# A planner's prices for the attention heads, and the place of the second image's attention and projections, in a two-layer vision kernel

## The chip, the cores and the metric

The kernel runs on one core of a Trainium2 chip. The metric is the device time of one execution in microseconds, as a median of several runs. Engines are named as the profile names them: PE (matrix products), DVE (vector), ACT (scalar, activations), POOL (GpSimd), SP (the queue that issues the DMAs).

## The reference

Two images of 48 x 48 positions with 768 channels, all in fp32, pass through two layers with a residual each:

```
x = x + attention(gn(x))       # 12 heads of 64; each position sees a 7 x 7 neighbourhood
x = x + mamba(gn(x))           # a selective scan over the 2304 positions, forwards and backwards
```

`gn` normalizes over 32 groups of channels and needs the sums over a whole image before the first position can be normalized. The attention computes q, k and v with a 768 x 2304 weight, masked softmax scores, the weighted sum, and an output product. The second layer projects each position to 1536 channels (u) and 1536 gates (z), convolves u with four taps in either direction, projects u to 48 + 16 + 16 values (a step size, B and C), and runs for each of the 1536 channels and 16 states the recurrence `h = exp(d*A)*h + d*u*B`, `y = sum(h*C)`, once over the positions in order and once in reverse. The sum of both, gated by `silu(z)`, goes through an output product of 1536 x 768.

## The kernel before

**The main work.** The scan is cut into 24 passes (2 images x 2 directions x 6 chunks of 384 positions), and each pass into 12 tiles of 128 channels: 288 *channel tiles*, numbered 0 to 287, image 1 from 144. One tile (`scan`, lines 1209 to 1389) has four groups of four states. For each group, `first` (L1254) fills a buffer with d*u*B, on DVE or POOL, whichever the planner finds sooner free; ACT computes exp(d*A) (L1276); DVE runs two scans over two states each (L1287); POOL multiplies by C (L1302); PE adds the states up by transposing into a PSUM bank (L1319); ACT takes the result out (L1345). `deltas_of` prepares three tiles at a time, with a POOL product at L1204.

**The jobs beside it.** Image 0's attention and the projections of its first chunk come ahead of tile 0. All else is laid beside the scans: image 0's other projections, image 1's attention, image 1's projections (`in_proj`: PE products, three DVE taps per tile and direction at L964, ACT silu at L990), the products for B and C (`x_proj`, which stores them to DRAM as `xdf` and `xdb`), and the output products (`out_proj`).

**The planner.** No instruction is issued when its Python line runs. `add(engine, ns, fn, key, r, w, job=...)` records a step with an engine, a planned duration in ns, what it reads and writes, and a *key*: the number of the channel tile beside which it belongs. `Order.run` then plays the steps through: each engine takes the step that can start first by the planned durations, ties going to the lower key, and a step whose key is more than 2.5 above the oldest unfinished main step is not yet open. The order that comes out is the program order of each engine, and SP's order of DMAs with it. On the chip the engines are in order and synchronized by semaphores. So a planned duration changes no instruction; it changes where instructions stand. If PE is planned to be idle for more than 800 ns in a scan, the planner fills the gap with idle transposes (L1520, `idle`), which keep PE running and compute nothing that is used.

**The prices.** `act(n, p) = 60 + 90p + 0.833n` and `dve(n) = 55 + 1.042n` ns, plus an amount by hand; a PE step's price is multiplied by 1.04 ahead of tile 0 and by 1.05 from there.

**The heads.** `heads` (L769 to L900) does one pair of heads for two blocks of 64 queries: scores on PE (L784), per block masked scores on DVE (L794) and exponentials on ACT (L800), reciprocals on DVE (L815), the scaling of the probabilities (L843 on ACT in image 1, L849 on DVE in image 0), their transposes on PE (L825), the copy out of PSUM (L831), the product with v (L879) and the copy of the result (L893). There are 108 such calls per image. `job` is true for image 1, whose attention lies beside the scans. The output product of the attention is `mm_ao`, followed on DVE by the residual sum (L712) and the statistics for the second group norm (L717).

**The places.** `attention(b, start, end, ...)` spreads its six blocks of rows evenly between two keys, and the second group norm has the key `end`. The chunks of `in_proj` of image 1 have their keys from `P1` in fixed steps; chunk i spans 10 tiles, its `x_proj` stands behind it, and the forward scan of chunk i starts at tile 144 + 12 i. A chunk's scan loads its `dt` and its B and C from `xdf`; these DMAs stand on SP's queue.

Of the kernel before, what the change touches and what calls it, by code (L numbers as in the profile page):

```python
# [16 lines left out]
P = 128  # L17
# [13 lines left out]
NKEY = WR * WC  # L31
KR = 7
KCH = tuple((r * WC, KR * WC) for r in range(0, WR, KR))
NK = len(KCH)
UU = 2
# [215 lines left out]
def tile_kernel(  # L251
# [3 lines left out]
    nc = tc.nc  # L255
# [99 lines left out]
    def dve(n):  # L355
        return 55 + n * 1.042
# [177 lines left out]
    def attention(b, start, end, job, T):  # L534
# [234 lines left out]
        def heads(n, p, i, u, kcs, ks, qs, vs, vat, mask, to, key):  # L769


            sc, pt = one("s", n), one("pt", n)
            pr = sb("pr", [P, UU, NKEY], n, parts=UU)
            pT = sb("pT", [P, UU, NK, P], n, parts=UU)
            sm = sb("sm", [P, 2 * UU], n, parts=2 * UU)
            grid = lambda h, kc: ks[h, i * WR * HW : (i + 1) * WR * HW].rearrange("p (r w) -> p r w", w=HW)[:, :, kc : kc + WC]
            scv = lambda v: bank(sc, UU * NKEY)[:, v * NKEY : (v + 1) * NKEY]

            def scores():
                for v in range(UU):  # L780
                    for j in range(2):
                        h = slice(j * E, (j + 1) * E)
                        at = (u * UU + v) * NQ
                        nc.tensor.matmul(  # L784
                            scv(v)[j * NQ : (j + 1) * NQ], qs[h, i, at : at + NQ], grid(h, kcs[v]),
                            start=True, stop=True,
                        )

            add("PE", mm(UU, NKEY) * 1.15, scores, key, r=[(ks, 0), qs], w=[sc, pr], **S)
            for v in range(UU):  # L790

                def masked(v=v):

                    nc.vector.tensor_tensor_reduce(  # L794
                        pr[:, v, :], scv(v), mask[:, v * NKEY : (v + 1) * NKEY], -1.0, 3.0e38,
                        ALU.add, ALU.min, sm[:, v : v + 1],
                    )

                def exponentials(v=v):
                    nc.scalar.activation(  # L800
                        pr[:, v, :], pr[:, v, :], AF.Exp, bias=sm[:, v : v + 1], scale=-1.0,
                        accum_out=sm[:, UU + v : UU + v + 1],
                    )

                add("DVE", dve(NKEY) + 160, masked, key, r=[sc, mask], w=[(pr, v), (sm, v)], **S)
                add(
                    "ACT", act(NKEY, 1) + 230, exponentials, key, r=[(pr, v), (sm, v)],
                    w=[(pr, v), (sm, UU + v)], **S,
                )

                if v == UU - 1 or not job:
                    of = range(UU if job else UU + v, UU + v + 1)
                    add(
                        "DVE", 198,
                        lambda of=of: nc.vector.reciprocal(  # L815
                            sm[:, of.start : of.stop], sm[:, of.start : of.stop]
                        ),
                        key, r=[(sm, of)], w=[(sm, of)], **S,
                    )

            def turned(vs):
                for v in vs:
                    for k, (c0, nk) in enumerate(KCH):
                        x = (v * NK + k) * P
                        nc.tensor.transpose(  # L825
                            bank(pt, UU * NK * P)[:nk, x : x + P], pr[:, v, c0 : c0 + nk], ident
                        )

            def taken(vs, copy):
                nk = KCH[0][1]  # L830
                copy(  # L831
                    pT[:nk, vs.start : vs.stop],
                    bank(pt, UU * NK * P)[:nk, vs.start * NK * P : vs.stop * NK * P].rearrange(
                        "p (v k q) -> p v k q", k=NK, q=P
                    ),
                )

            for v in range(UU):
                if job:

                    add(
                        "ACT", act(NKEY, 1) + 40,
                        lambda v=v: nc.scalar.mul(pr[:, v, :], pr[:, v, :], sm[:, UU + v : UU + v + 1]),  # L843
                        key, r=[(pr, v), (sm, UU + v)], w=[(pr, v)], **S,
                    )
                else:
                    add(
                        "DVE", 300,
                        lambda v=v: nc.vector.tensor_scalar_mul(  # L849
                            pr[:, v, :], pr[:, v, :], sm[:, UU + v : UU + v + 1]  # L850
                        ),
                        key, r=[(pr, v), (sm, UU + v)], w=[(pr, v)], **S,
                    )
            if job:
                add("PE", UU * NK * 110 + 60, lambda: turned(range(UU)), key, r=[pr], w=[pt, pT], **S)
                add(
                    "ACT", act(UU * NK * P) + 30, lambda: taken(range(UU), nc.scalar.copy), key, r=[pt],
                    w=[pT], **S,
                )
            else:  # L860
                for v in range(UU):
                    add(
                        "PE", NK * 120 + 60, lambda v=v: turned([v]), key,
                        r=[(pr, v), *([pt] if v else [])], w=[pt, (pT, v)], **S,
                    )
                for v, (eng, copy) in enumerate((("ACT", nc.scalar.copy), ("DVE", nc.vector.tensor_copy))):
                    add(
                        eng, act(NK * P) + 60, lambda v=v, copy=copy: taken(range(v, v + 1), copy), key,
                        r=[pt], w=[(pT, v)], **S,
                    )  # L870
            po = ps(tag("po", p), f"po{n}")

            def weighted():

                for v in range(UU):
                    for k, (c0, nk) in enumerate(KCH):
                        for j in range(2):
                            e0 = i * P + j * E
                            nc.tensor.matmul(  # L879
                                po[j * E : (j + 1) * E, v * NQ : (v + 1) * NQ],  # L880
                                vat(v, k, nk, e0, e0 + E), pT[:nk, v, k, j * NQ : (j + 1) * NQ],
                                start=k == 0, stop=k == NK - 1,
                            )

            marks["pv"] = add(
                "PE", 900, weighted, key, r=[*((x[0], x[1]) for x in vs), pT], w=[po, to], **S
            )
            o, oi = to

            def kept():  # L890
                copy = nc.scalar.copy if job else nc.vector.tensor_copy
                w0 = u * UU * QC
                copy(  # L893
                    o[:, oi, :]
                    .rearrange("p (r w) -> p r w", w=HW)[:, :, w0 : w0 + UU * QC]
                    .rearrange("p r (v c) -> p v r c", c=QC),
                    po[:, : UU * NQ].rearrange("p (v r c) -> p v r c", v=UU, r=QR),
                )

            add("ACT" if job else "DVE", act(P) + 60, kept, key, r=[po], w=[to], **S)  # L900

        project(0)
        for t in range(NTB):
# [5 lines left out]
    def in_proj(b, i, start, end, conv=True, gate=True, nk=KB, tags=("uz",), banks=("mm",), proj=None):  # L909
# [78 lines left out]
        def finish(k0, nk, uz, dsts, key):  # L988
            def silu():
                nc.scalar.activation(uz[:, :, :, :cl], uz[:, :, :, :cl], AF.Silu)  # L990
                nc.scalar.preload_act_table_set("natural_log_exp_and_others")

            add("ACT", 2600 + act(len(dsts) * nk * cl), silu, key, r=[uz], w=[uz], job=True)
            for s, dst in enumerate(dsts):
                add(
                    "SP", 400,
                    lambda s=s, dst=dst: nc.sync.dma_start(
                        rows_of(dst, k0, nk, l0, cl), uz[:, s, :, :cl]
                    ),
                    key + 0.1, r=[(uz, range(s * nk, (s + 1) * nk))],  # L1000
                    w=[(dst, cols(l0, cl, k0, nk))], job=True, size=nk * P * cl * 4,
                )
# [154 lines left out]
    def deltas_of(ch, k0, x):  # L1157
# [38 lines left out]
        for j in range(KB):  # L1196
# [3 lines left out]
                at + 0.03 + 0.25 * j, [(u, j)], [vts[j]], early=EARLY,  # L1200
            )
            add(
                "POOL", 960,
                lambda j=j: nc.gpsimd.tensor_mul(u[:, j, h], dl[:, j, c], u[:, j, h]), at + 0.06 + 0.25 * j,  # L1204
                [(dl, j), (u, j)], [(u, j)], early=EARLY,
            )
# [239 lines left out]
    LATE = 4  # L1446
    FIRM = 4.0
    HEAD = ("bc4", "bc5", "bc6", "bc7", "bc0", "bc1")
    A0, A1, P1 = (-56, -16), (50, 118), 118
    norms, norms0, stats = [], [], []  # L1450
    for b in range(nb):
        s0 = stats_of(b, A0[0] - 2 + 20 * b, b > 0, ("stage",) if b else ("xc", "uz"))
# [4 lines left out]
    for b in range(nb):  # L1457
# [1 line left out]
        if b:  # L1459
            attention(b, *A1, True, BESIDE)  # L1460
        for i in range(NCH):
            start = P1 + 12 * i if b else 9 * (i - 1) - 4
            end = start + (ND - 2 if b else 8)


# [105 lines left out]
```

## Time and profile before

| | |
|---|---|
| median of three runs | 7049.78 us (7040.85 to 7054.37) |
| the profiled execution | 7040.0 us, of which the span of the core is 7038.2 us |
| first scan tile's start | about 1020 us |
| tiles 0 to 287 | about 1020 to 7007 us |
| what follows (last output product) | 31 us |
| busy over the span | PE 89%, DVE 85%, POOL 78%, ACT 69% |
| granted PE clock, mean | 0.976 |
| idle transposes L1520 | 5124 |

In the profile a view of stretches gives each engine's busy time between two points of the execution. The points used here are the moments at which ACT takes out every twelfth tile's result (L1345), so a stretch is one pass of twelve tiles: 1301.4 us is the end of tile 11, 2841.6 that of tile 83, 3700.1 that of tile 119. A view of waits tells for each instruction that came after idle time which other instruction released it. PE's busy time counts pipelined matmuls by modelled ends, so it is close to full in many places where PE could still take work. An fp32 matmul of the program shows as two instructions in the trace, except for transposes.

### The profile page before, as it was taken

Reading aid. Unit: us, or ns where it says so; the run is one execution under the profiler, and the core shown is the slowest. Engines: PE = TensorE matmul, PEld = TensorE weight load, DVE = VectorE, ACT = ScalarE, POOL = GpSimd, SP = SyncE. Lnnn points to the kernel's source line nnn. Section 1 sums busy time; section 2 is a strip of 40 time slices with the busy share of each in tenths; the row PEclk is TensorE's granted clock in tenths of the full one; section 3 lists DMA queues with packets and bytes.
Section 4 is the critical chain, followed back from the end, with each engine's and each line's share of the span. In section 5 each row is a group of like instructions: output and inputs, shape, how many; then the busy total and the mean of one; then the engine's idle time right before and its main releaser. Section 6 shows DMA issues by size and latency. Waiting matters only on the chain. (4 is left out here: it accounts for less than half of the span.)

```text
span 7038.2 us, 108877 instructions
## 1 busy us (share of the span) xinstructions
PE 6280.1 (89%) x40140; PEld 4878.2 (69%) x40140; DVE 5990.5 (85%) x6102; ACT 4851.3 (69%) x10516; POOL 5468.5 (78%) x1958
## 2 busy tenths in 40 slices
PE   8999899899899989899988888888888898999888
PEld 5666656666667767666766666666678887777777
DVE  1343459999999989878899999999999999999998
ACT  1222248878887777677877777788876667777774
POOL 0000019898889989777889999999999999999997
PEclk9999999999999999999999999999999999999999
DMA  6666454544565455555542443343466676655553
GB/s 194 185 214 190 143 174 131 153 137 133 162 190 162 148 165 166 161 175 155 179 152 87 137 138 89 95 143 114 139 179 191 175 218 198 192 176 160 163 171 104
DMA packets 1348293, 1115.48 MB, mean 158 GB/s; under 512 B 137840, under 2 KB 1338000, under 8 KB 1347728
## 3 DMA queue, kind: packets, MB, share of 16 engines
q1 hardware_dynamic: 1347760, 1108.50, 52.6%
q8 instruction: 318, 5.21, 0.3%
q14 instruction: 215, 1.76, 0.1%
HBM read 895.34 MB, written 213.57 MB: 158 GB/s over the span
## 5 line engine op out<-in xcount | busy, mean ns | idle before, releaser
L1287 DVE TENSOR_TENSOR_SCAN hb<-da,hb 128x772 f32<-128x772 f32 x2304 | 3923.6, 1749 | 200.1 <-ACT da L1276 148.8
L1302 POOL TENSOR_TENSOR hb<-hb,bc 128x1536 f32<-128x1536 f32 x1152 | 3652.7, 3186 | 379.4 <-DVE hb L1287 287.9
L1276 ACT ACTIVATE da<-dlt,A 128x384 f32<-128x384 f32 x4608 | 2677.4, 584 | 962.5 <-DVE hb L1287 884.9
L1319 PE MATMUL py<-ident,hb 128*128 128x128 f32 x13824 | 1750.0, 279 | 313.5 <-POOL hb L1302 306.6
L1319 PEld LDWEIGHTS py<-ident,hb 128*128 128x128 f32 x13824 | 1566.1, 143 | 570.5 <-POOL hb L1302 471.7
L1254 POOL TENSOR_TENSOR hb<-u,bc 128x1544 f32<-128x1544 f32 x502 | 1606.8, 3203 | 48.7 <-PE py L1319 42.6
L1254 DVE TENSOR_TENSOR hb<-du,bc 128x1544 f32<-128x1544 f32 x650 | 1131.3, 1746 | 37.3 <-ACT du L1231 27.5
L1204 POOL TENSOR_TENSOR u<-dlt,u 128x384 f32<-128x384 f32 x288 | 263.6, 917 | 478.0 <-ACT dlt L1191 386.9
L1520 PE MATMUL py<-ident 128*128 128x128 f32 x5124 | 630.8, 277 | 0.0
L387 PE MATMUL mm_xin<-xc,w_x 128*128 128x390 f32 x1656 | 592.6, 501 | 29.8 <-DVE uz_u L964 12.6
L387 PE MATMUL mm_z<-xc,w_z 128*128 128x384 f32 x1728 | 607.6, 492 | 6.3 <-ACT dlt L1186 3.8
L1520 PEld LDWEIGHTS py<-ident 128*128 128x128 f32 x5124 | 586.8, 143 | 17.3 <-issue 13.6
L387 PE MATMUL mm_out<-stage_y,w_o 128*128 128x192 f32 x3168 | 558.0, 330 | 18.9 <-DMA w_o<-in_w_opT 6.5
L387 PEld LDWEIGHTS mm_out<-stage_y,w_o 128*128 128x128 f32 x3168 | 519.0, 193 | 30.5 <-ACT dlt L1186 10.6
L930 POOL MEMSET xc<- 128x18 f32 x4 | 0.5, 118 | 630.0 <-PE mm_v L387 630.0
L964 DVE SCALAR_TENSOR_TENSOR uz_u<-mm_xin,conv_w,uz_u 128x384 f32<-128x384 f32 x792 | 427.9, 610 | 45.6 <-ACT uz_u L957 44.0
L387 PEld LDWEIGHTS mm_xin<-xc,w_x 128*128 128x128 f32 x1656 | 306.3, 193 | 230.2 <-issue 28.8
L387 PE MATMUL mm_qk<-xc_xn,w_qk 128*128 128x384 f32 x1296 | 452.8, 495 | 8.7 <-DVE sm L794 2.6
L387 PEld LDWEIGHTS mm_z<-xc,w_z 128*128 128x128 f32 x1728 | 314.8, 192 | 192.4 <-issue 9.4
L387 PEld LDWEIGHTS mm_qk<-xc_xn,w_qk 128*128 128x128 f32 x1296 | 238.6, 192 | 161.8 <-issue 15.9
L1260 ACT COPY bc<-state 128x8 f32<-128x8 f32 x960 | 183.0, 196 | 143.9 <-DVE hb L1254 68.3
L800 ACT ACTIVATE pr<-pr,sm 128x196 f32<-128x196 f32 x432 | 194.0, 450 | 126.4 <-DVE sm L794 124.8
(163 smaller groups left out, 6454.8 us busy)
## 6 DMA issues: line engine op xcount, KB each, us to landing
w_o<-in_w_opT SPq DMA_DIRECT2D x264, 384.0 KB
bc<-xdf SPq DMA_DIRECT2D x96, 768.0 KB
bc<-xdb SPq DMA_DIRECT2D x96, 768.0 KB
w_qk<-in_w_qkv SPq DMA_DIRECT2D x144, 384.0 KB
w_x<-in_w_inT SPq DMA_DIRECT2D x144, 384.0 KB
w_z<-in_w_inT SPq DMA_DIRECT2D x144, 384.0 KB
w_ao<-in_w_out SPq DMA_DIRECT2D x72, 384.0 KB
u<-uf SPq DMA_DIRECT2D x48, 576.0 KB
```

Of the source, the lines that this page charges most:

```text
L387: nc.tensor.matmul(acc[:m, o0 : o0 + cl], wb[:, wi, wo : wo + m], xb[:, xi, xo : xo + cl], start=c == 0, stop=c == n - 1,)
L800: nc.scalar.activation(pr[:, v, :], pr[:, v, :], AF.Exp, bias=sm[:, v : v + 1], scale=-1.0, accum_out=sm[:, UU + v : UU + v + 1],)
L930: nc.gpsimd.memset(xc[:, :, : a - lo], 0.0)
L964: nc.vector.scalar_tensor_tensor(u, px[:, at[j] : at[j] + cl], q["conv_w"][:, k, j : j + 1], u, ALU.mult, ALU.add,)
L1204: lambda j=j: nc.gpsimd.tensor_mul(u[:, j, h], dl[:, j, c], u[:, j, h]), at + 0.06 + 0.25 * j,
L1254: on.tensor_mul(cells(hb, SG), by.unsqueeze(1).to_broadcast([P, SG, W]), bc[g].ap)
L1260: "ACT", 98, lambda: nc.scalar.copy(bc[g][:, :, ends], was), now - 0.4,
L1276: lambda: nc.scalar.activation(cells(da, 2)[:, j % 2, h], dl[:, jd, c], AF.Exp, scale=q["A"][:, k, i : i + 1]),
L1287: lambda: nc.vector.tensor_tensor_scan(flip(hb[at2]), flip(da[:, : 2 * W]), flip(hb[at2]), 0.0, ALU.mult, ALU.add),
L1302: lambda: nc.gpsimd.tensor_mul(cells(hb, SG)[:, :, h], cells(hb, SG)[:, :, h], bc[NSG + g][:, :, c]),
L1319: nc.tensor.matmul(py[:tp, t * P : (t + 1) * P], cells(hb, SG)[:, j, h][:, tb[t]], ident, start=False, stop=g == NSG - 1 and j == SG - 1 a ...
L1520: nc.tensor.matmul(marks["py"][:, CL : CL + P], ident, ident, start=False, stop=False, is_transpose=True, skip_group_check=True,)
```

## The change

Two kinds of numbers in the planner's input change. First, prices of the attention's steps: masked scores 419 to 281 ns, exponentials 543 to 443, the reciprocals 198 to 70 (image 1) or 150 (image 0), the scaling on ACT 353 to 348, the copy of the transposes in image 1 516 to 486, the product with v 900 to 640 (image 1) or 750 (image 0), the copy of its result 227 to 167 on ACT and 227 to 230 on DVE. Beside them, every silu of the projections is priced 150 ns higher, and the POOL product at L1204 850 instead of 960 ns. Second, places: image 1's attention is keyed from tile 46 to tile 124 instead of 50 to 118, its group norm therefore at 124, and the projections of its six chunks start at keys 124, 135, 146, 157, 168, 179 instead of 118, 130, 142, 154, 166, 178.

```diff
-                add("DVE", dve(NKEY) + 160, masked, key, r=[sc, mask], w=[(pr, v), (sm, v)], **S)
+                add("DVE", dve(NKEY) + 22, masked, key, r=[sc, mask], w=[(pr, v), (sm, v)], **S)
                 add(
-                    "ACT", act(NKEY, 1) + 230, exponentials, key, r=[(pr, v), (sm, v)],
+                    "ACT", act(NKEY, 1) + 130, exponentials, key, r=[(pr, v), (sm, v)],
...
-                        "DVE", 198,
+                        "DVE", 70 if job else 150,
                         lambda of=of: nc.vector.reciprocal(
...
-                        "ACT", act(NKEY, 1) + 40,
+                        "ACT", act(NKEY, 1) + 35,
...
-                    "ACT", act(UU * NK * P) + 30, lambda: taken(range(UU), nc.scalar.copy), key, r=[pt],
+                    "ACT", act(UU * NK * P), lambda: taken(range(UU), nc.scalar.copy), key, r=[pt],
...
-                "PE", 900, weighted, key, r=[*((x[0], x[1]) for x in vs), pT], w=[po, to], **S
+                "PE", 640 if job else 750, weighted, key, r=[*((x[0], x[1]) for x in vs), pT], w=[po, to], **S
...
-            add("ACT" if job else "DVE", act(P) + 60, kept, key, r=[po], w=[to], **S)
+            add("ACT" if job else "DVE", act(P) if job else 230, kept, key, r=[po], w=[to], **S)
...
-            add("ACT", 2600 + act(len(dsts) * nk * cl), silu, key, r=[uz], w=[uz], job=True)
+            add("ACT", 2750 + act(len(dsts) * nk * cl), silu, key, r=[uz], w=[uz], job=True)
...
-                "POOL", 960,
+                "POOL", 850,
                 lambda j=j: nc.gpsimd.tensor_mul(u[:, j, h], dl[:, j, c], u[:, j, h]), at + 0.06 + 0.25 * j,
...
-    A0, A1, P1 = (-56, -16), (50, 118), 118
+    A0, A1, P1 = (-56, -16), (46, 124), 124
...
-            start = P1 + 12 * i if b else 9 * (i - 1) - 4
+            start = P1 + 11 * i if b else 9 * (i - 1) - 4
```

## Prediction

> **What bounds the kernel now.** I began with the page: busy shares and the forty slices.
>
> ```profile
> PE 6280.1 (89%) x40140; PEld 4878.2 (69%) x40140; DVE 5990.5 (85%) x6102; ACT 4851.3 (69%) x10516; POOL 5468.5 (78%) x1958
> ...
> PE   8999899899899989899988888888888898999888
> ...
> DVE  1343459999999989878899999999999999999998
> ...
> POOL 0000019898889989777889999999999999999997
> ```
>
> Until slice 6 the kernel has no scan and PE alone is busy. From then on DVE and POOL are nearly full, but for a dent in slices 16 to 20. There image 1's attention runs beside the scans. The chain that ended last reaches back only to 4498 us, so it says nothing of that dent; I went on to the view of stretches of twelve tiles (columns: length, then busy time and instructions of PE, PE's weight loads, DVE, ACT, POOL, then clock, DMA share, GB/s).
>
> ```profile
> 0.00:1020.00 1020.00, 925.40 (x5669) 627.04 (x5670) 376.59 (x1397) 265.02 (x734) 5.59 (x15) 0.96 0.61 185
> ...
> 2563.20:2841.60 278.40, 248.58 (x1846) 187.76 (x1846) 248.06 (x279) 218.17 (x534) 237.47 (x85) 0.96 0.51 159
> 2841.60:3148.50 306.90, 284.58 (x1866) 205.53 (x1867) 249.92 (x283) 219.81 (x560) 240.71 (x86) 0.98 0.55 167
> 3148.50:3425.80 277.30, 257.73 (x1983) 203.44 (x1981) 228.33 (x249) 207.82 (x529) 219.99 (x79) 0.96 0.53 167
> 3425.80:3700.10 274.30, 239.72 (x1955) 182.80 (x1955) 245.66 (x322) 218.93 (x585) 221.17 (x80) 0.96 0.50 152
> 3700.10:3956.20 256.10, 215.27 (x1402) 170.28 (x1402) 246.85 (x217) 195.81 (x401) 242.05 (x86) 0.99 0.37 114
> 3956.20:4204.30 248.10, 208.22 (x1401) 169.63 (x1401) 241.86 (x206) 186.01 (x348) 238.83 (x85) 0.96 0.41 126
> ```
>
> The last two rows (tiles 120 to 143) show the kernel at its bound: DVE idles 9.2 and 6.2 us. In the four rows before (tiles 72 to 119) it idles 30.3, 57.0, 49.0 and 28.6 us, 164.9 of 1136.9. The worst, 84 to 95, is also the one where PE is fullest, 93%. The waits of that stretch say why:
>
> ```profile
> DVE xr_x L712 <- PE mm_ao L387: 11.7, 6, 3.3
> DVE zs L1382 <- PE mm_yb L1372: 8.0, 1, 8.0
> DVE hb L1254 <- PE py L1319: 5.6, 6, 1.8
> DVE ev L607 <- PE mm_qk L387: 5.2, 4, 2.7
> ...
> POOL hb L1254 <- PE py L1319: 28.7, 6, 8.3
> POOL hb L1302 <- DVE hb L1287: 25.7, 16, 5.4
> ```
>
> DVE waits 30.5 us for PE in these four rows, and POOL 28.7 us for PE to free a scan buffer. So there the bound is PE, elsewhere DVE and POOL, and ahead of tile 0 PE again (925 of 1020 us).
>
> **The change: prices.** The chip's instructions are the same ones; by the order of the two built programs only the idle transposes (5124 to 5076) and one `first` that goes from DVE to POOL differ in number. Whether the new prices are nearer to the chip is read from a timeline of image 1's heads (start, duration):
>
> ```profile
> 2893.12 0.35 DVE L794 CUSTOM_DVE_ANT_0 pr<-mm_s,mask 128x196 f32<-128x196 f32 x1
> ...
> 2893.40 0.36 DVE L794 CUSTOM_DVE_ANT_0 pr<-mm_s,mask 128x196 f32<-128x196 f32 x1
> ...
> 2893.52 0.46 ACT L800 ACTIVATE pr<-pr,sm 128x196 f32<-128x196 f32 x1
> ...
> 2893.98 0.44 ACT L800 ACTIVATE pr<-pr,sm 128x196 f32<-128x196 f32 x1
> ...
> 2901.48 4.14 PE L387 MATMUL mm_ao<-stage_oT,w_ao 128*128 128x384 f32 x12
> ```
>
> What counts is start to start: 280 ns for the masked scores (priced 419, now 281) and 460 for the exponentials (543, now 443). The plan had held engines longer than the chip does: per head of image 1 on DVE 2 x 138 + 128 = 404 ns, on ACT 2 x 100 + 2 x 5 + 30 + 60 = 300, on PE 260 x 1.05 = 273; over 108 heads 44, 32 and 29 us. None of that is time on the chip. What it can buy is an order with fewer waits. I read how much PE work the order puts between a head's scores and its transposes, the room its softmax has: for image 1 the median rises from 5.9 to 6.8 us, and the heads with under 4 us fall from 20 to 10 of 108. Over the whole trace PE idles 8.4 us at these transposes for L843, 6.9 for L893, and 10.1 and 6.1 at L879 for the copy L831, 31.5 in all. If a third of it goes, that is 10 us of PE, and as PE sets the pace in part of the stretch alone, I take -4 us; ends 0 and -31.5.
>
> For image 0 the same reading moves little: under 3 us 37 to 43 heads, pairs of heads with back-to-back transposes 28 to 32, and each such pair waits 1.0 us for the copy L831 to free the bank (the group PE L825 from DVE L831: 20.1 us, 21 times). Transposes that the order splits with a product between fall from 16 to 4. PE's work ahead of tile 0 is the same instructions. I take 0; ends +20 (that wait once more) and -20 (it vanishes).
>
> **The change: places.** Counted in the order of both programs, per twelve tiles from 72 (before, after): program matmuls of q and k, 78, 120, 72, 0 and 84, 90, 84, 12; of the attention's output product, 36, 72, 36, 72, 0 (to tile 131) and 36, 54, 54, 36, 36. Heads' masked scores, four to a head by rows: 76, 96, 88, 124, 0 and 64, 92, 72, 120, 24. Twelve rows of 128x384, six program matmuls, took 4.14 us, 0.69 each.
> - Tiles 84 to 95 lose 30 + 18 = 48 matmuls, 33 us of PE, and 2.7 us of DVE (three L712, three L717, a copy, two heads' halves, one `first` more). What they become looks like the row of tiles 96 to 107: there PE and DVE have the work that 84 to 95 will have (counted by start-to-start times, PE 237 and 237, DVE 245 and 246 us). That row took 277.3, so 306.9 becomes about 277: -30. Ends 0 and -57, DVE's idle time. Next late after PE is DVE itself waiting for the exponentials of the scan (L1276, 14.3 us here).
> - Tiles 96 to 107: PE -9, DVE -6 us: -7. Tiles 108 to 119: DVE -8, among it the group norm's aggregates: -8. Ends 0 and -20 each.
> - Tiles 120 on: the work goes to stretches at the bound, so every us counts in full. By counts times start-to-start durations (`first` and scan 1.66 us on DVE, taps 0.525, POOL's `first` 3.16), the fuller of DVE and POOL gets +7 in 120 to 131 (six heads and six L712 come, 30 taps go, five `first` come to DVE), +6, -5, +7, 0 and +6 in the next five, +3 from 192 on. Together +24. Before tile 84 the sums cancel to within 1 us.
>
> On SP's queue every `xdf` store and load of image 1 moves: the second store of chunk 0 stood ten tiles ahead of the load (129 to 139) and now stands two ahead (137, 139); chunk 1 three (148, 151), the others six to eight. A load that waits there holds back all u, weight and gate loads behind it. Two tiles are about 42 us; the DMAs land within a few us, so I take 0; the price if it fails stands below.
>
> Sum: -4 - 30 - 7 - 8 + 24 = -25. The profiled execution took 7040.0, 9.8 below the median of the runs shown; so 7015 for such an execution and 7025 as a median.
>
> [...]
>
> **The rivals.**
> - *More of the dent fills.* If tiles 84 to 107 come down to the idle share of DVE in 108 to 119, 28.6 of 274.3 or 10.4%, they take (249.9 + 228.3 - 9) / 0.896 = 524 instead of 584 us, -60 in place of -37; with ten more ahead of tile 0 and four in 72 to 83 the sum is -62, 6988. For it: the plan's new prices touch just these heads. Against: two of these rows still have more PE work than 108 to 119.
> - *Given back in full.* DVE and POOL pass buffers to each other, and 25.7 us of POOL's waits in 84 to 95 are for DVE. If half the -30 stays away, the 24 us of work moved to full stretches eat the rest: -10, 7040; with none of it +5, 7055. About 7050.
> - *Slower: projections too late.* Attention ends four tiles later and the projections run closer together. If heads and taps bring to tiles 120 to 155 the idle share of 108 to 119, these 755.7 us go from 21.8 idle to 10.4%, 57 more: -25 + 57 = +32, 7082. For it: the margin of two tiles above; the stretches are full. Against: all stores still stand ahead of their loads. It decides where chunk 0's second store comes later than two tiles after its place.
>
> **How the numbers follow.** Forecast 0.43, the first rival 0.14, given back 0.17, slower 0.26. The order is dealt anew in all stretches, and those of like work differ in DVE's idle time by 4.5 to 13.4 us, which spreads every case by some 20 us. The range reaches from the first rival, 6985, to the last, 7080. About 0.2%, 14 us, is what a measurement of this kernel can tell: faster is below 7036, slower above 7064. The forecast and first rival give faster 0.57 (the forecast's spread to the right stands against that of the third case to the left), same 0.16, slower 0.27. The likeliest case has its own range, 7000 to 7045.
>
> **What would show it.** Right: the stretch of tiles 84 to 95 shorter by 20 us or more with PE under 90% busy, the waits of POOL L1254 for PE there below 15 us, tiles 120 to 191 longer by some 20 us together, the first scan again near 1020 us. A slight loss of clock may come with it: in rows where PE is less full it is 0.96, in the full one 0.98, 2% of some 250 us of PE, 5 us of an engine that then bounds less. Wrong: an unchanged 84 to 95 (PE was not the bound), SP waiting at `dt` or B and C loads around tile 144, or a head that ends later than 1040 us.

## The result, and the profile after

The changed kernel takes 7054.76 us (median of 12 runs) against 7050.62 us (12 runs): ratio 1.0005, 95% interval 0.9997 to 1.0012. No change. The profiled executions are 7057.13 and 7040.0 us, spans 7055.4 and 7038.2. The profiled execution of the kernel before lies 10.6 us under its median and that of the changed kernel 2.4 over its own, so the traces show a difference of 17 us where the medians show 4. The equal totals hide large movements. The stretches of the changed kernel, cut again at every twelfth tile (tiles 72 to 143 in the last six rows; the first row is the part ahead of tile 0):

```profile
0.00:1058.60 1058.60, 931.47 (x5679) 629.92 (x5680) 373.27 (x1398) 267.02 (x736) 6.39 (x15) 0.96 0.59 179
2606.20:2863.00 256.80, 231.29 (x1712) 174.58 (x1710) 242.41 (x254) 206.30 (x498) 236.82 (x84) 0.99 0.56 173
2863.00:3143.40 280.40, 259.63 (x1776) 191.06 (x1776) 239.88 (x261) 211.09 (x536) 228.96 (x83) 0.96 0.54 166
3143.40:3410.50 267.10, 246.26 (x1726) 184.23 (x1727) 243.06 (x265) 210.19 (x537) 234.49 (x84) 0.98 0.56 170
3410.50:3671.70 261.20, 232.61 (x2044) 182.76 (x2042) 223.16 (x293) 216.07 (x576) 224.74 (x80) 0.99 0.48 152
3671.70:3945.40 273.70, 232.53 (x1566) 184.25 (x1567) 258.34 (x239) 193.07 (x429) 232.30 (x85) 0.95 0.36 110
3945.40:4198.30 252.90, 212.00 (x1415) 169.78 (x1413) 244.36 (x212) 190.22 (x348) 242.37 (x86) 0.98 0.40 122
```

The head is 38 us longer with the same instructions: the first scan starts at 1058.6 instead of 1020.8 us, PE busy 931.5 of it in place of 926.2 and idle 127.1 in place of 94.6. The four stretches of the dent are shorter by 21.6, 26.5, 10.2 and 13.1 us; the first behind it is longer by 17.6. In five parts (the output product's end, the last 31 and 33 us, is left out), with DVE's idle time:

| us | head | tiles 0-47 | 48-119 | 120-191 | 192-287 |
|---|---|---|---|---|---|
| before | 1020.8 | 1079.3 | 1600.1 | 1493.4 | 1813.5 |
| after | 1058.6 | 1089.7 | 1523.4 | 1535.2 | 1815.4 |
| difference | +37.8 | +10.4 | -76.7 | +41.8 | +1.9 |
| DVE idle before, after | | 74, 89 | 198, 141 | 46, 66 | 61, 66 |

The dent gave more than was forecast for it, and the head took half of that back. What PE waited for in the head, first before, then after:

```profile
PE mm_gna L453 <- DVE gn_mva L448: 28.3, 1, 28.3
PE da L825 <- DVE pT L831: 20.1, 21, 1.0
PE py_po L879 <- DMA bc_v<-vd: 11.5, 25, 1.7
PE da L825 <- DVE sm L815: 4.9, 5, 2.3
PE da L784 <- DVE sm L794: 3.1, 6, 1.0
```

```profile
PE da L825 <- DVE pT L831: 28.3, 28, 1.5
PE mm_gna L453 <- DVE gn_mva L448: 28.1, 1, 28.1
PE py_po L879 <- DMA bc_v<-vd: 24.1, 37, 5.3
PE da L784 <- DVE sm L794: 15.1, 21, 0.8
PE da L825 <- DVE pr L849: 4.6, 14, 0.8
```

Three rows grew: transposes waiting until the copy L831 has emptied their bank (+8.2 us), products with v waiting for the load of v (+12.6), and scores waiting until the masked scores L794 have read the bank (+12.0, 21 times instead of 6): 32.8 us, as much as PE's idle time grew (32.5). The copies and the masked scores themselves take 424 and 358 ns before and 423 and 358 after; by these rows the plan put PE's steps too soon behind what they need. The other 5.3 of the 37.8 us are busy time of PE for the same instructions, on which the last section has more.

In tiles 84 to 95 most of the waits that carried the forecast are gone. POOL's, after, and two of DVE's:

```profile
POOL hb L1302 <- DVE hb L1287: 30.9, 13, 6.5
POOL u L1204 <- ACT vt L1199: 16.3, 2, 15.0
...
POOL hb L1254 <- PE py L1319: 0.5, 1, 0.5
```

```profile
DVE pr L794 <- PE mm_s L784: 8.8, 4, 6.6
...
DVE xr_x L712 <- PE mm_ao L387: 2.4, 1, 2.4
```

POOL L1254 waits 0.5 us for PE where it had waited 28.7. DVE waits 7.0 for PE in the four groups that had been 30.5 (now L712 2.4, L607 2.4, L1254 1.8, L1382 0.4), but its masked scores, L794, wait 8.8 for the scores, where it had been 0.7: 15.8 in place of 31.2 in all. A new row came, POOL L1204 behind ACT's L1199, 16.3 us.

### The profile page after: what moved, and what is told of

It reads as the page before. It is cut to its first block, busy times and chain, and to the rows that moved or that the text cites. A ratio compares the mean times of both kernels' runs of the same rounds, so it can differ in the third digit from the quotient of the medians.

```text
span 7055.4 us, 108816 instructions
## 1 busy us (share of the span) xinstructions
PE 6281.7 (89%) x40092; PEld 4869.4 (69%) x40092; DVE 5981.3 (85%) x6101; ACT 4845.1 (69%) x10516; POOL 5470.9 (78%) x1959
## 4 chain that ended last, share of the span: by engine, by line
DVE 38%; PE 20%; ACT 15%; POOL 12%; issue 9%; DMA 5%; SPq 1%; DVEq 0%; POOLq 0%; ACTq 0%
DVE hb L1287 25%; POOL hb L1302 8%; DVE hb L1254 7%; ACT da L1276 4%; PE mm_qk L387 4%; DVE uz_u L964 3%; POOL hb L1254 3%; PE py L1319 3%; PE mm_v L387 2%; PE mm_ao L387 2%; PE mm_xin L387 2%; DMA bc_v<-vd 1%; PE da L784 1%; ACT L1192 1%; ACT L1191 1%
## 5 line engine op out<-in xcount | busy, mean ns | idle before, releaser
L1254 POOL TENSOR_TENSOR hb<-u,bc 128x1544 f32<-128x1544 f32 x503 | 1611.0, 3205 | 25.1 <-PE py L1319 23.8
L1254 DVE TENSOR_TENSOR hb<-du,bc 128x1544 f32<-128x1544 f32 x649 | 1129.1, 1746 | 53.1 <-ACT du L1231 32.9
L1204 POOL TENSOR_TENSOR u<-dlt,u 128x384 f32<-128x384 f32 x288 | 263.8, 917 | 534.1 <-ACT dlt L1191 408.4
L387 PEld LDWEIGHTS mm_qk<-xc_xn,w_qk 128*128 128x128 f32 x1296 | 241.9, 195 | 162.0 <-issue 15.1
L1180 PE MATMUL mm_dl<-dt,dtw 49*128 49x384 f32 x576 | 252.0, 538 | 38.9 <-ACT dlt L1186 15.1
```

The lines of the kernel that those rows point to most:

```text
L387: nc.tensor.matmul(acc[:m, o0 : o0 + cl], wb[:, wi, wo : wo + m], xb[:, xi, xo : xo + cl], start=c == 0, stop=c == n - 1,)
L1180: lambda j=j, acc=acc: nc.tensor.matmul(acc[:, c], w[:, j * P : (j + 1) * P], dt[:, c], start=True, stop=True),
L1254: on.tensor_mul(cells(hb, SG), by.unsqueeze(1).to_broadcast([P, SG, W]), bc[g].ap)
```

## The experiments

Ratios are to the kernel before on the same chip. The three batches of four ran on three chips, on which the kernel before had medians of 7055.20, 7050.33 and 7057.31 us, so across batches the ratios are compared and not the medians; an interval reaches some 10 us to either side. The parts are read from one profiled execution each. In every kernel only the planner's input differs, so all do the same work, but for idle transposes, in another order. First the two halves of the change, and the head alone.

**e1, the new prices alone**

```diff
 (against the changed kernel, whose price lines all stay)
-    A0, A1, P1 = (-56, -16), (46, 124), 124
+    A0, A1, P1 = (-56, -16), (50, 118), 118
-            start = P1 + 11 * i if b else 9 * (i - 1) - 4
+            start = P1 + 12 * i if b else 9 * (i - 1) - 4
```

> The new prices alone, image 1's attention and projections at their old places. Its order is that of the changed kernel up to tile 49, so the head should end near 1058 us and tile 47 near 2148 us, 48 us behind the kernel before. Theory A (the places filled the dent of tiles 48 to 119 and cost tiles 120 to 191; the prices only cost the head): the dent stays near 1600 us, tiles 120 to 191 near 1493, total about 7050 + 48 = 7098. Theory B (the prices filled the dent): tiles 48 to 119 near 1523 us, total about 7050 + 48 - 77 = 7021.

**e2, the new places alone**

```diff
 (against the kernel before)
-    A0, A1, P1 = (-56, -16), (50, 118), 118
+    A0, A1, P1 = (-56, -16), (46, 124), 124
-            start = P1 + 12 * i if b else 9 * (i - 1) - 4
+            start = P1 + 11 * i if b else 9 * (i - 1) - 4
```

> The new places alone, with all old prices. Its order is that of the kernel before up to tile 51: head near 1020 us, tile 47 near 2100 us. Theory A (places fill the dent): tiles 48 to 119 near 1523 us, tiles 120 to 191 near 1535, total about 7050 - 77 + 42 = 7015. Theory B (prices fill it): dent near 1600 us, tiles 120 to 191 up by 20 to 40, total 7070 to 7090.

**e3, the changed kernel with image 0's heads at the old prices**

```diff
 (against the changed kernel)
-  dve(NKEY) + 22, masked                  +  dve(NKEY) + (22 if job else 160), masked
-  act(NKEY, 1) + 130, exponentials        +  act(NKEY, 1) + (130 if job else 230), exponentials
-  70 if job else 150,                     +  70 if job else 198,
-  640 if job else 750, weighted           +  640 if job else 900, weighted
-  act(P) if job else 230, kept            +  act(P) if job else act(P) + 60, kept
```

> The changed kernel, but with image 0's heads at their old prices; image 1's prices and all places are new. Ahead of tile 0 its order is that of the kernel before. Theory H (the new prices of image 0's heads cost the head 38 us of PE waits, and all behind it follows): head ends near 1020 us, total about 7055 - 38 = 7017. Rival (an earlier first scan is lost again behind it, since the order of the later stretches is dealt anew): total within 7040 to 7060.

**e4, the kernel before with image 0's heads at the new prices**: the same five lines the other way round.

> The kernel before, with the new prices for image 0's heads alone. Ahead of tile 0 its order is that of the changed kernel. Theory H: head ends near 1058 us and nothing else changes much, total about 7050 + 38 = 7088. Rival (the loss of the head is made up later): 7050 to 7065.

| | median | ratio (95%) | head | 0-47 | 48-119 | 120-191 | 192-287 |
|---|---|---|---|---|---|---|---|
| before | 7055.20 | | 1020.8 | 1079.3 | 1600.1 | 1493.4 | 1813.5 |
| e1 prices | 7091.91 | 1.0048 (1.0032-1.0064) | 1057.1 | 1089.9 | 1571.8 | 1509.8 | 1828.4 |
| e2 places | 6997.27 | 0.9920 (0.9906-0.9935) | 1024.8 | 1085.7 | 1524.2 | 1522.3 | 1808.0 |
| e3 | 7034.85 | 0.9968 (0.9955-0.9981) | 1031.7 | 1095.1 | 1525.5 | 1534.2 | 1813.4 |
| e4 | 7076.73 | 1.0028 (1.0018-1.0038) | 1057.1 | 1079.2 | 1603.2 | 1492.2 | 1817.1 |

The two halves have opposite signs, both clear: the places alone are 0.8% faster than the kernel before, the prices alone 0.5% slower. e2's parts come near its theory A, at a total 18 us better. e1 lies between its theories in the dent, 1571.8 us, and loses beside the head (36 us) 11 us in tiles 0 to 47, 16 in 120 to 191 and 15 behind. With old prices the places bring the dent to 1524.2, as low as the whole change does, and cost 29 us in tiles 120 to 191. The prices without the places take 28 us from the dent, which they don't give beside the places (e2 and the changed kernel: 1524.2 and 1523.4); that the two fill the same idle time would explain it and isn't shown. e3 and e4 put the head's loss on image 0's heads: with their new prices 1057.1, with the old ones 1031.7. e3's total missed its number by 18 us (7035 for 7017): 11 of them in the head, which came at 1031.7 for 1020, and 5 in tiles 0 to 47. e4's total, +21.5, lies between its two expectations, though its profiled execution has the full 36 us in the head and nothing elsewhere. So the head's loss is smaller in the medians than in the traces: 0.28%, 20 us, in e4, and 0.37%, 26 us, from e3 to the changed kernel.

That left e3 38 us behind e2, though both have the old head: something in the rest of the prices costs time. The next four start from e2 and add one price or one group of prices each.

**e5, the POOL product's price**

```diff
-                "POOL", 960,
+                "POOL", 850,
```

> The new places with old prices (6997 us, tile 47 at 2110 us), and of the new prices only that of the POOL product at L1204, 850 instead of 960 ns. Every kernel with all new prices needed 1090 to 1095 us for tiles 0 to 47, every one without them 1079 to 1086; only this price and that of the silu act there. Theory: this price costs those 5 to 15 us, total 7002 to 7012. Rival (it is the silu's price, or the head's end): tiles 0 to 47 stay at 1079 to 1086, total 6990 to 7002.

**e6, image 1's heads**: the change's price lines for `job` alone (281, 443, 70, 348, 486, 640, 167), image 0 as before.

> The new places with old prices, and of the new prices only those of image 1's heads. The order is the one of the run with new places up to where image 1's heads begin. Theory R (in the dent the prices matter little once the places are spread, and an order with less room for the heads costs a little behind): tiles 48 to 119 near 1525 us, tiles 120 to 191 within 1520 to 1540, total 6997 to 7015. Rival (prices that fit the chip give an order with fewer waits, as the prediction took): tiles 48 to 119 down to 1510 or less, total 6985 or less.

**e7, image 0's product with v**

```diff
-                "PE", 900, weighted
+                "PE", 900 if job else 750, weighted
```

> The new places with old prices, and for image 0's heads the product with v at 750 instead of 900 ns, nothing else. Theory S (the head's 36 us come from the softmax prices, with which the scores and transposes are placed too close behind DVE): first scan within 1018 to 1030 us, total 6990 to 7005. Rival V (they come from the product with v, whose loads then are waited for: 24 us instead of 12 in the changed kernel): first scan near 1050 us, total near 7025.

**e8, image 0's softmax**

```diff
-  dve(NKEY) + 160, masked             +  dve(NKEY) + (160 if job else 22), masked
-  act(NKEY, 1) + 230, exponentials    +  act(NKEY, 1) + (230 if job else 130), exponentials
-  "DVE", 198,                         +  "DVE", 198 if job else 150,
```

> The new places with old prices, and for image 0's heads the new prices of the masked scores, the exponentials and the reciprocals alone. Theory S: first scan at 1045 to 1060 us, PE's waits for L794 before the scores 10 us or more instead of 3, total 7020 to 7035. Rival V: first scan near 1025 us, total near 6997.

| | median | ratio (95%) | head | 0-47 | 48-119 | 120-191 | 192-287 |
|---|---|---|---|---|---|---|---|
| e5 POOL | 7017.47 | 0.9955 (0.9938-0.9972) | 1021.9 | 1086.0 | 1537.4 | 1525.8 | 1811.2 |
| e6 image 1 | 6981.25 | 0.9902 (0.9887-0.9917) | 1028.3 | 1080.4 | 1510.9 | 1517.6 | 1810.1 |
| e7 v, image 0 | 7011.15 | 0.9936 (0.9918-0.9954) | 1029.1 | 1080.9 | 1527.2 | 1528.5 | 1817.1 |
| e8 softmax, image 0 | 7044.89 | 0.9995 (0.9985-1.0006) | 1072.6 | 1078.8 | 1526.8 | 1525.5 | 1809.2 |

The head's loss is the softmax prices (theory S): 1072.6 us, with the product with v at its old price. PE's idle time there is 129.0 us, as in the changed kernel (127.1) and against 96.4 in e2; of the 14 us by which this head is longer than the changed kernel's, 12 are busy time of PE for the same work (943.6 against 931.5 us). The head and the total, 7045, are both over what theory S expected. e8's waits in the head:

```profile
PE da L825 <- DVE pT L831: 30.3, 30, 1.3
PE mm_gna L453 <- DVE gn_mva L448: 28.5, 1, 28.5
PE py_po L879 <- DMA bc_v<-vd: 25.9, 42, 5.3
PE da L784 <- DVE sm L794: 13.4, 18, 0.8
```

e7 has the row of v's loads at 23.9 us as well, but its row of the copy L831 falls to 15.7, and its head is not late. So the loads' row alone is not the loss. e7's total, 7011, missed its range, though its head, 1029.1, kept to it; 9 us of that stand in tiles 192 to 287, where its order is e2's.

e6 came where its rival put it: image 1's prices, beside the new places, take 13 us from the dent and 5 behind it, 0.18% or 13 us by the ratios, whose intervals overlap. The dent of e2 and of e6:

```profile
2110.50:3634.70 1524.20, 1387.63 (x10006) 1063.96 (x10006) 1371.40 (x1392) 1200.11 (x2949) 1356.80 (x484) 0.98 0.54 164
2108.70:3619.60 1510.90, 1371.73 (x9901) 1052.85 (x9903) 1385.04 (x1402) 1206.37 (x2954) 1329.95 (x474) 0.98 0.55 166
```

DVE idles 27 us less, and half of that is work that came over from POOL: 172 `first` on DVE and 115 on POOL, where e2 has 163 and 124. PE's waits that the prediction had priced, at the transposes for L843 and L893 and at L879 for L831, did not fall: 24.8 us in e2, 25.3 in e6.

e5 missed its place. The POOL price leaves tiles 0 to 47 at 1086.0, as e2 has it, and costs 13 us in the dent; the total is 0.35%, 25 us, above e2 by the ratios.

The last four start from e6.

**e9, the silu's price**

```diff
-            add("ACT", 2600 + act(len(dsts) * nk * cl), silu, ...
+            add("ACT", 2750 + act(len(dsts) * nk * cl), silu, ...
```

> The best kernel so far (new places, new prices for image 1's heads, 6981 us) with the silu priced at 2750 instead of 2600 ns. The kernels with all new prices took 1090 to 1095 us for tiles 0 to 47, where image 0's silus stand, the others 1079 to 1086, and the POOL price alone left them at 1086. Theory: it is the silu's price, tiles 0 to 47 take 1088 to 1095 us, total 6988 to 7000. Rival (it needs both prices, or is the spread of a new order): 1079 to 1086 us, total 6975 to 6990.

**e10, new durations, old delays** (`tail` is what the planner adds until a result may be used; the engine is free before it)

```diff
-  add("DVE", dve(NKEY) + (22 if job else 160), masked, ...)
+  y = add("DVE", dve(NKEY) + 22, masked, ...)
+  y.tail += 0 if job else 138
 (likewise the exponentials: + 130, tail + 100; the reciprocals: 150, tail + 48)
```

> The same best kernel, with image 0's softmax steps at their new durations, but with what was taken off each (138, 100 and 48 ns) added to the planned delay after which another step may use its result. So an engine is planned to be free as early as in the changed kernel, and a result to be there as late as in the kernel before. Theory L (the old prices stood for the delay until a result is usable, and the changed kernel lost that room): first scan back at 1018 to 1032 us, PE's waits for L794 before the scores under 6 us, total near 6981. Rival O (the engines' planned occupation matters): first scan at 1060 to 1075 us, total near 7025. Half back would say that both count.

**e11, a nudge**

```diff
-  dve(NKEY) + (22 if job else 160), masked    +  dve(NKEY) + (22 if job else 161), masked
-  "POOL", 960,                                +  "POOL", 961,
```

> The same best kernel with two prices changed by 1 ns, which can mean nothing for the chip: image 0's masked scores 420 for 419, the POOL product 961 for 960. It measures what dealing the order anew does by itself. If the order is robust: each of the five parts (head, tiles 0 to 47, 48 to 119, 120 to 191, 192 to 287) within 5 us and the total 6976 to 6987. If the deal is a lottery of the size of the effects found: parts off by 10 to 40 us, total outside 6970 to 6995.

**e12, more room**

```diff
-  (22 if job else 160), masked           +  (22 if job else 298), masked
-  (130 if job else 230), exponentials    +  (130 if job else 330), exponentials
-  70 if job else 198,                    +  70 if job else 246,
```

> The same best kernel with image 0's softmax steps priced still higher, by as much as the change had lowered them: masked scores 557, exponentials 643, reciprocals 246 ns. Theory L, carried on (room is what counts, and the old prices already gave enough): first scan within 1010 to 1035 us, PE's waits before L784 and L825 no more than before, total 6965 to 6990. Rival (any price off the old one deals a worse head): first scan later than 1045 us, total 7000 or more.

| | median | ratio (95%) | head | 0-47 | 48-119 | 120-191 | 192-287 |
|---|---|---|---|---|---|---|---|
| e9 silu | 7003.75 | 0.9923 (0.9909-0.9938) | 1021.4 | 1087.0 | 1527.1 | 1524.5 | 1812.3 |
| e10 tails | 7009.27 | 0.9935 (0.9919-0.9952) | 1045.4 | 1082.5 | 1511.1 | 1522.0 | 1812.3 |
| e11 nudge | 6995.72 | 0.9911 (0.9896-0.9926) | 1036.5 | 1079.2 | 1514.8 | 1521.0 | 1815.3 |
| e12 room | 6981.55 | 0.9890 (0.9875-0.9905) | 1023.8 | 1083.3 | 1511.7 | 1517.5 | 1812.3 |

e11 was meant to deal the order anew, and did not: in its trace PE, DVE and POOL run e6's order, by line and tile, from start to end. So it shows how far executions of one order differ. Other kernels repeat an order too. In seven heads (before, e2, e3, e5, e6, e9, e11) PE has one order, and they end between 1020.8 and 1036.5 us. Behind the head e4 has the order of the kernel before, e3 that of the changed kernel, e7 and e8 that of e2, and e10, e11 and e12 that of e6; within such a group the four parts differ by up to 7, 4, 6 and 9 us. Effects of that size in a part say nothing here. The dents of e2's order, 1524.2 to 1527.2, and of e6's, 1510.9 to 1514.8, are apart by more. e11's total missed its range and stands 14 us above e6's in the medians, 0.09% or 6 us by the ratios, with the same order; a total alone doesn't tell an effect of 10 us.

By that measure the silu's price costs time in the dent, 12 us more than the longest of e6's order, and nothing that can be told in tiles 0 to 47 (1087.0 us, just under its expectation). With e5 both prices, the silu's and the POOL product's, do harm, 0.21% and 0.35% or 15 and 25 us by the ratios, in a part where neither was looked for. Why a plan with them is worse there the runs don't say. Both deal the order anew from tile 5 on, and as the nudge dealt nothing, no run shows whether another price moved as far would have cost the same.

e10 gives some six tenths of the head's loss back: 1045.4, between 1028.3 of e6 and 1072.6 of e8, with PE idle for 107.8 us, between 95.2 and 129.0. The waits of the scores are halved:

```profile
PE mm_gna L453 <- DVE gn_mva L448: 28.1, 1, 28.1
PE py_po L882 <- DMA bc_v<-vd: 24.5, 32, 4.2
PE da L828 <- DVE pT L834: 22.7, 25, 1.0
PE da L784 <- DVE sm L794: 6.2, 11, 1.0
```

(Lines below 805 stand three to four higher in this kernel.) So part of what the old prices stood for is the delay until a result can be used. The other part then goes with the occupation, the one thing that e10 leaves changed, and theory L holds for about six tenths only. e12 raises the prices once more and loses nothing: head 1023.8, the waits of L825 for the copy down to 11.4 us, those of L784 to 2.3:

```profile
PE py_po L879 <- DMA bc_v<-vd: 19.2, 35, 1.3
PE da L825 <- DVE pT L831: 11.4, 11, 1.6
...
PE da L784 <- DVE sm L794: 2.3, 4, 1.0
```

Between e6 and e12 there is no difference that their intervals tell. Both beat the kernel before and the changed one by about 1%. e12's row of v's loads is longer than e6's (19.2 for 13.4 us), and PE's idle time in its head is the same (96.3 and 95.2).

## Why the prediction was right or wrong

The forecast of 7025 was not what came, but the range held it. I had given a faster kernel 0.57 and an unchanged one 0.16, and the unchanged one came. Its time is that of the second rival, given back in full (about 7050), by another way: that rival let the -30 stay away, and the dent in fact gave more than forecast. That the range held is luck. The head lost more than the end I had set it, tiles 0 to 47 lost 10 us for which I had no term, and a gain of 27 us in tiles 48 to 83, which I had not seen either, made up for much of it. A head that ends later than 1040 us I had named as a sign of being wrong, and it came.

- **The dent, right in the main.** PE was the bound of tiles 84 to 95. I had called it the row where PE is fullest, but the next row is as full (92.9% to 92.7%), so the waits carry this reading, not the share. With 33 us of PE moved out, the stretch fell from 306.9 to 280.4 (forecast 277), PE's share stayed at 93% of the shorter stretch, where I had named under 90% as a sign, and POOL's wait for PE from 28.7 to 0.5 us. Tiles 84 to 119 gave 49.8 us against 45 forecast. I had written that the sums before tile 84 cancel; tiles 48 to 83 gave another 27, idle time that no count of work shows. e2, with 1524.2 us for tiles 48 to 119, says that the places do all of this.
- **The waits and the share of the weight loads.** PE's weight loads took 67% of that stretch before (205.5 of 306.9 us) and 68% after (191.1 of 280.4), while POOL's wait for PE went from 28.7 to 0.5 us. For the question who holds up whom at a given place the waits were a better reading than that share.
- **Work moved to full stretches, right in kind, short in size.** I had +21 us for tiles 120 to 191 (the other 3 lay behind); measured +41.8 in the whole change, +29 with the places alone. DVE's busy time rose by 21.5 us, just that term (1447.8 to 1469.3); the rest is its idle time there, 46 to 66 us: the third rival's mechanism in small, 3.1% to 4.3% idle instead of 10.4%. (Divided out as in the first rival, that rival's 57 us would have been 63.) The late projections did not bite: no load of `dt` is among SP's waits from 3900 to 4700 us, and its waits at the B and C loads are for buffers, not for `xdf`.
- **The head, wrong.** The step that failed is "For image 0 the same reading moves little ... I take 0; ends +20 and -20". The head lost 38 us in the traces, 20 to 26 in the medians, and it is the softmax prices (e4, e8). The counts I read pointed the right way, 37 to 43 heads with under 3 us of room and 28 to 32 pairs back to back, and were too coarse: they left out the wait of the scores for the bank, which made 12 us, and the loads of v.
- **Prices for image 1, right in sign by luck.** I had -4, from a third of PE's 31.5 us of waits at the transposes and the product with v. These waits stayed, 30.2 us in the changed kernel. e6 gives -13 beside the new places, by an order in which DVE idles less; what in the new prices makes that order is open.
- **Prices without a term.** The silu's and the POOL product's new prices had none in my sum, as I had looked whether they fit the trace and not what order they make. They cost some 15 and 25 us (e9, e5). Neither alone lengthens tiles 0 to 47 beyond what equal orders differ by, so the 10 us there stay open.
- **The clock, misread.** I had 0.98 for the row where PE is full and 0.96 for less full ones. The next row, as full, has 0.96, and the two emptiest have 0.99 and 0.96, so these rows show no such relation.

Added up from the ratios of the runs, each a difference of two: places -56 us, image 1's prices -13, silu +15, POOL +25, image 0's heads +20 (e4) to +53 (e8 against e2). That is -9 to +24, and +4 was measured. On one chip without such a sum: e2 is 58 us faster than the kernel before, e3, with all new prices but those of image 0's heads, 38 slower than e2, and these last prices take the rest. What was argued and not shown is why the silu's and the POOL product's prices do harm.

## What to carry to other kernels

A duration in a planner isn't a description of the chip but a control of the order. If it holds an instruction's throughput alone (here 281 ns for masked scores that take 358 each), the planner can place dependent steps too soon behind what they need, and the engine then waits, as PE did in the head at the scores for 15.1 us in place of 3.1. An old price that looks too high may be the room which that chain needs: in e10 the delays alone brought some six tenths of the head's loss back. So shorten the planned occupation apart from the delay of the result, and change one price at a time. And a total that stays the same is no proof that nothing happened: cut both traces at the same work, here every twelfth tile, before judging; in the traces a loss of 38 us stood beside a gain of 77. And before a nudge is taken for a yardstick of a new order, see in the trace that the order did change.

## What the runs showed of the hardware

The granted clock of PE differed between executions of the same order, and it showed in the time where PE was the bound. The heads of the kernel before, of e2, e6 and of e11 have one order of PE and end at 1020.8, 1024.8, 1028.3 and 1036.5 us, with a mean granted clock of 0.96, 0.96, 0.96 and 0.95. The rows of the kernel before and of e11 up to there:

```profile
0.00:1020.80 1020.80, 926.20 (x5672) 627.54 (x5673) 377.36 (x1398) 265.02 (x734) 6.39 (x15) 0.96 0.61 185
```

```profile
0.00:1036.50 1036.50, 936.73 (x5677) 635.14 (x5678) 378.08 (x1398) 266.07 (x736) 6.37 (x15) 0.95 0.60 182
```

By the clock's records the granted clock was 0.5 for 75, 82, 89 and 102 us of these four; half of the 27 us between the first and the last is 14 of the 16 us by which their heads differ. The other three heads with this order (e3, e5, e9) have 89, 82 and 79 us; with half of that time taken off, each of the seven ends between 981 and 987 us. In e8, where PE waits most, it is 123 us at a mean of 0.94, and PE's busy time for the same work is 15 us longer than in e2 (943.6 to 928.4), so by estimate, from these 15 us and half of the 41 us more at 0.5, 15 to 20 us of that head's 48 are the clock and not the wait itself. In the changed kernel it is 85 us, half of whose 10 us above the kernel before are the 5 us by which PE is busy longer.

In the head of the kernel before, the records hold a clock of 1.0 and, eleven times, one of 0.5, for 3.4 us or a multiple of it up to 13.7. No gap between PE's matmuls from 100 to 1020 us is longer than 2.3 us. In the 3.4 us before each of the eleven PE was idle for 0.8 to 2.2 us in all, in ten of them for more than 1 us; of the 247 other stretches of that length from 60 us on that ran at 1.0 and were followed by 1.0, six have over 1 us of idle time.
